# Graph attention on Trainium2: a second of the first projection's seven half-size products also made of seven smaller ones

## The chip, the cores and the metric

The kernel runs on one core of one Trainium2 chip. The metric is the device time of one execution in microseconds (us). Three runs of the kernel before took 2768.26, 2771.11 and 2773.03 us; the median is 2771.11 us.

## What is computed

The reference applies two graph attention layers to 32 graphs of 512 nodes with 512 features, after a layer norm and a relu, and adds the input. The first layer has 4 heads of 256 features that are set side by side (W1 is 512x1024), the second one head of 512 (W2 is 1024x512). All of it is in float32.

```python
def gat_layer(x, mask, W, a_src, a_dst, bias, concat):
    B, N, _ = x.shape
    H, F = a_src.shape
    xl = (x @ W).reshape(B, N, H, F)
    asrc = jnp.einsum('bnhf,hf->bnh', xl, a_src)
    adst = jnp.einsum('bnhf,hf->bnh', xl, a_dst)
    e = jax.nn.leaky_relu(asrc[:, :, None, :] + adst[:, None, :, :], 0.2)
    e = jnp.where(mask[..., None], e, -1e9)
    attn = jax.nn.softmax(e, axis=1)
    out = jnp.einsum('bsdh,bshf->bdhf', attn, xl)
    out = out.reshape(B, N, H * F) if concat else out.mean(axis=2)
    return out + bias

mask = (adj > 0) | eye(512)
h = maximum(layernorm(x), 0)
h = elu(gat_layer(h, mask, W1, att_src1, att_dst1, b1, concat=True))
h = gat_layer(h, mask, W2, att_src2, att_dst2, b2, concat=False)
return x + h
```

## The kernel before

**Sevens.** Each graph has four large products: the first projection (h times W1), the first gather (weights of attention times the projected features, by head), the second projection and the second gather. All but those of the first graph, and the last gather, are done by the scheme of Strassen and Winograd: left and right are cut into 2x2 blocks, sums of blocks are formed, and seven products of blocks take the place of eight. Call the left blocks a11 to a22 and the right ones b11 to b22. The left sums are s1 = a21 + a22, s2 = s1 - a11, s4 = a12 - s2 and a21 = a11 - a21 (in place); the right ones t1 to t4. Product 1 is a11 b11, 2 is a12 b21, 3 is s4 b22, 4 is a22 t4, 5 is s1 t1, 6 is s2 t2, 7 the new a21 times t3. Products that share an output block accumulate in PSUM; a copy by ScalarE or an add by VectorE carries one into another block. The sums of the weights are made once, in `w1_sb` and `w2_sb`; those of the left side for each graph, by VectorE (`sums`, into `hs` and `hs4`).

**The first projection** (`project1`) has four units: two halves of 128 rows in each row block, times two pairs of heads. Per unit and product there are two matmuls, over the two halves of 128 of the block's depth, each with 256 + 2 columns (the two extra ones carry the attention scores). The units are worked on in two groups of two (`ORDER1`), at different places in the program.

**The smaller sevens.** `SMALL = (5,)` names the products of the first projection that are themselves cut into 2x2 and made of seven. Their left blocks are 128x128, their right blocks 128x129, and each small product is one matmul of 129 columns. Product 5 takes 7 matmuls in a group in place of 8 of 258 columns. `small_left` makes the left sums in a buffer `hx` (VectorE, three sums there and one in place), `sums_of_small_weights` the right ones in `wx`, once. `step` in `sevens` emits small product q of one group, in the order 5, 1, 2, 6, 3, 7, 4:

- 5 goes to the upper half of a bank of PSUM that the smalls use by themselves (`tt`), and ScalarE copies it to a buffer `e` (a slot `f`): the shared piece.
- 1 goes to the lower half of that bank, and ScalarE copies it to the first unit's bank; 2 is accumulated there, and 6 on top of 1 in the lower half.
- After 6, VectorE adds the lower half and `e` into the upper half of the first unit's bank, where 3 is accumulated. 7 is accumulated in the lower half, and VectorE adds it and `e` into the second unit's bank. 4 is accumulated in the lower half, and ScalarE copies that to the second unit's bank.

The result of product 5 or 1 is then copied by ScalarE to `xl` or to a second bank, as if it had come from whole matmuls (`done`).

**Order.** `Program` records each operation as a job with its engine, an assumed cost and the keys it reads and writes; from the keys it derives what a job must wait for. The jobs repeat for 30 middle graphs, a "turn" each of 470 jobs: gather 1 and projection 2 of one graph, projection 1 of the next, gather 2 of the one before, and the loads, masks and norm ahead. `PLACES` is a table with a number for each job of the start, of one turn and of the tail. Before, `order` runs a simulation in which each engine takes the ready job with the lowest number, with assumed costs, latencies between engines (`PAIRS`, `CROSS`) and DMA queues that slow each other (`KIND`, `LATE`). The jobs are emitted in the order that comes out, so each engine's sequence is fixed.

**Elsewhere on the way.** `norm` forms the mean and variance of the four tiles of a graph (VectorE), then one POOL power for all four. `norm_turn` applies norm and relu (ScalarE) and turns the tile: for graphs 0 and 1 by TensorE with the identity `identf`, for the others by DMA. The first graph's projection is done plainly (`project1_first`); its weights carry attention scores in two columns, which `scores1` makes with VectorE products from the loads of `att_src1` and `att_dst1` (into `p0`). `xr` is a ring of buffers for the exp of `elu` on ScalarE, which VectorE reads.

Of the kernel before, what the change touches and what calls it, by code (L numbers as in the profile page):

```python
# [10 lines left out]
F32 = mybir.dt.float32  # L11
# [8 lines left out]
P = 128  # L20
EPS = 1e-5
# [23 lines left out]
class Banks(Slots):  # L45
# [171 lines left out]
)  # L217
LATE = {
   
}  # L220


class Program:
# [51 lines left out]
    def kind(self, j):  # L275

        if self.jobs[j][0] == "POOL":
            return self.MASK
# [1431 lines left out]
```

## Time and profile before

| | |
|---|---|
| median of three runs | 2771.11 us (2768.26 to 2773.03) |
| profiled execution, its own time | 2769.33 us |
| its span in the trace | 2767.6 us |
| mean granted clock of TensorE | 0.999 |
| matmuls in the program | 6480, seen as 12924 records |
| operations of VectorE, of ScalarE (records) | 6732, 4907 |
| DMA | 502.14 MB, mean 181 GB/s |

The span runs from the first to the last instruction of the profiled execution. An engine's busy time is the sum over its records, where a float32 matmul shows as two records on TensorE ("PE") with two weight loads ("PEld"). In the groups, a name such as `mm<-wx,hx` reads "to mm, from wx and hx", without the buffers' numbers; L531 is the line of TensorE's helper, L517 that of VectorE's (DVE), L514 that of ScalarE's (ACT). What follows an arrow in a row of idle time is the instruction whose end ended it.

### The profile page before, as it was taken

What the parts mean: (1) busy time and instruction counts of PE and PEld (TensorE: products, weight loads), DVE (VectorE), ACT (ScalarE), POOL (GpSimd) and SP (SyncE); (2) the same over time, 40 slices, a digit from 0 to 9 for tenths busy, and PEclk for the clock granted to TensorE, in tenths of its full rate; (3) what the DMA queues carried; (4) which work ended last, traced back from release to release, by engine and by line L of the source; (5) the groups of instructions that cost most, each with busy time, mean ns of one, the idle gap of its engine ahead of it and who ended that gap; (6) DMA issues with size and microseconds to landing.
All of it is one profiled execution on the core that took longest, in us unless ns stands there. A gap on an engine that the chain in (4) does not pass through costs nothing. (4 is left out here: it accounts for less than half of the span.)

```text
span 2767.6 us, 42320 instructions
## 1 busy us (share of the span) xinstructions
PE 2742.4 (99%) x12924; PEld 2371.8 (86%) x12924; DVE 2558.2 (92%) x6732; ACT 2229.1 (81%) x4907; POOL 313.1 (11%) x356
## 2 busy tenths in 40 slices
PE   7999999999999999999999999999999999999999
PEld 6788888888888888888888888888888888888887
DVE  8999999999999999999999999999999999999996
ACT  5978888778887788877888877888778788788883
POOL 0110111101111111111011111111111111101110
PEclk9999999999999999999999999999999999999999
DMA  8657766667666667667676766766676767767563
GB/s 232 176 157 182 203 167 184 187 176 194 182 183 179 182 176 196 178 175 195 173 201 172 182 187 178 192 186 180 180 188 175 201 167 180 195 165 208 162 171 112
DMA packets 375864, 502.14 MB, mean 181 GB/s; under 512 B 222804, under 2 KB 227668, under 8 KB 375636
## 3 DMA queue, kind: packets, MB, share of 16 engines
q1 hardware_dynamic: 329844, 332.68, 42.4%
q0 software_dynamic: 45792, 166.74, 25.1%
q8 instruction: 103, 1.69, 0.3%
q14 instruction: 125, 1.02, 0.1%
HBM read 316.41 MB, written 51.31 MB: 133 GB/s over the span
## 5 line engine op out<-in xcount | busy, mean ns | idle before, releaser
L531 PE MATMUL mm<-w_sb,hs 128*128 128x257 f32 (+3 forms) x2908 | 667.0, 367 | 5.1 <-ACT mm L514 3.3
L531 PEld LDWEIGHTS mm<-w_sb,hs 128*128 128x128 f32 x2908 | 539.7, 190 | 87.7 <-ACT mm L514 6.7
L525 POOL DMA_DIRECT2D p<-dm x314 | 273.2, 875 | 2295.0 <-DVE p L517 764.3
L531 PE MATMUL mm<-w_sb,ht 128*128 128x258 f32 x2112 | 528.6, 382 | 2.7 <-ACT mm L514 2.5
L531 PE MATMUL mm<-p,xl 128*128 128x258 f32 (+1 forms) x1984 | 495.8, 383 | 0.1
L531 PE MATMUL mm<-w_sb,h 128*128 128x257 f32 x2056 | 477.8, 379 | 0.0
L517 DVE SCALAR_TENSOR_TENSOR p<-rr,z 128x512 f32<-128x512 f32 (+1 forms) x636 | 456.0, 742 | 2.4 <-DMA rr<-drr 2.4
L531 PEld LDWEIGHTS mm<-w_sb,ht 128*128 128x128 f32 x2112 | 393.7, 190 | 63.6 <-ACT mm L514 6.4
L514 ACT ACTIVATE p<-p,z 128x512 f32<-128x512 f32 (+1 forms) x636 | 433.4, 720 | 17.7 <-DVE p L517 12.4
L531 PEld LDWEIGHTS mm<-w_sb,h 128*128 128x128 f32 x2056 | 389.0, 189 | 58.4 <-ACT xl L514 0.5
L531 PEld LDWEIGHTS mm<-p,xl 128*128 128x128 f32 x1984 | 367.2, 190 | 52.7 <-issue 6.0
L514 ACT ACTIVATE mm<-mm 128x257 f32<-128x257 f32 (+2 forms) x498 | 169.8, 347 | 269.2 <-PE mm L531 236.2
L514 ACT ACTIVATE l<-as,z 128x512 f32<-128x512 f32 x516 | 354.4, 716 | 30.8 <-DMA as<-das 30.7
L514 ACT ACTIVATE l<-l,low 128x512 f32<-128x512 f32 x516 | 370.3, 721 | 7.6 <-DVE low L517 6.7
L517 DVE CUSTOM_DVE_ANT_1 l<-l,mt 128x512 f32<-128x512 f32 x516 | 346.2, 681 | 28.4 <-ACT l L514 27.4
L514 ACT ACTIVATE xl<-mm 128x258 f32<-128x258 f32 (+2 forms) x748 | 269.3, 382 | 91.4 <-PE mm L531 89.8
L514 ACT ACTIVATE h<-mm,b_sb 128x256 f32<-128x256 f32 (+1 forms) x504 | 231.0, 480 | 77.3 <-PE mm L531 76.6
L531 PE MATMUL mm<-t,hs 128*128 128x258 f32 (+1 forms) x992 | 246.1, 380 | 0.0
L517 DVE TENSOR_TENSOR xl<-xl,mm 128x258 f32<-128x258 f32 x372 | 155.3, 419 | 57.9 <-PE mm L531 48.3
L531 PEld LDWEIGHTS mm<-t,hs 128*128 128x128 f32 x992 | 185.8, 190 | 25.5 <-DVE t L517 0.2
L531 PE MATMUL mm<-xl,p 128*128 128x258 f32 (+2 forms) x752 | 189.7, 388 | 1.0 <-ACT h L514 0.6
L517 DVE SCALAR_TENSOR_TENSOR h<-xr,h 128x512 f32<-128x512 f32 x256 | 172.2, 683 | 6.1 <-ACT xr L514 6.1
(137 smaller groups left out, 3706.2 us busy)
## 6 DMA issues: line engine op xcount, KB each, us to landing
p<-dm POOLq DMA_DIRECT2D x314, 512.0 KB, 5.0
rr<-drr SPq DMA_DIRECT2D x159, 512.0 KB
x<-in_x_dram SPq DMA_DIRECT2D x129, 256.0 KB
adj<-in_adj_dram SPq DMA_DIRECT2D x128, 256.0 KB
as<-das SPq DMA_DIRECT2D x64, 512.0 KB
t<-in_x_dram SPq DMA_DIRECT2D x124, 256.0 KB
out_dram<-t SPq DMA_DIRECT2D x124, 256.0 KB
dm<-m SPq DMA_DIRECT2D x64, 256.0 KB
```

Source lines behind the costliest of these rows:

```text
L514: prog.add("ACT", cost, reads, writes, lambda: nc.scalar.activation(*a, **k))
L517: prog.add("DVE", cost, reads, writes, lambda: f(*a, **k))
L525: lambda: nc.gpsimd.dma_start(to, at, accum_op=OP.add), size,
L531: f(*a, **k)
```

## The change

Product 1 of the first projection is also made of seven smalls, each of 129 columns (`SMALL = (1, 5)`). Per projection 8 matmuls of 258 columns go and 14 of 129 come. `ORDER1` is unchanged in its text, and gives the smalls of the two products by turns: 5 of product 1, 1 of product 1, 5 of product 5, 1 of product 5, then 2 and 6, 3 and 7, and 4.

Space is found for the second set of buffers in three ways. The shared piece `e` has no slot `f` any more: it is laid in `hx`, where s1 was, once small product 5 has read it. So s1 is formed again (`again`, s2 + a11) between the two groups of a projection. The identity lies in `hx` of product 1 until that product's first sum is made. The ring `xr` has two buffers in place of three. The parts of `hx` have keys of their own.

The norm of the first graph goes tile by tile, with a POOL power for each, where one served all four.

The simulation in `order` is gone: the jobs stand on each engine in the order of their numbers in a new `PLACES`, and a turn has 496 jobs.

```diff
 PLACES = (
-    -21124, -21123, -21187, -21124, -19956, -19941, -19942, -21301, -19903, -19904, -18841, -19897, -6146, 6511,
...
+    -5190682, -5178775, -5187057, -5178772, -5178769, -5191242, -5141726, -5033531, -4987115, -5012829,
...
     def order(self):
-        jobs, rank = self.jobs, self.ranks()
...
+        lines = {e: [] for e in self.ENGINES}
+        for j in sorted(range(len(jobs)), key=lambda j: (rank[j], j)):
+            lines[jobs[j][0]].append(j)
+        lines = [deque(q) for q in lines.values()]
+        while any(lines):
+            q = min((q for q in lines if q and not left[q[0]]), key=lambda q: rank[q[0]])
+            j = q.popleft()
             done.append(j)
...
-    SMALL = (5,)
+    SMALL = (1, 5)
...
-    hx = {n: sbuf.tile([P, 3, P], F32, name=f"hx{n}") for n in SMALL}
+    hx = {n: sbuf.tile([P, 3 * P + 1], F32, name=f"hx{n}") for n in SMALL}
+    identf = hx[SMALL[0]][:, :P]
+    make_identity(nc, identf)
...
-    fs = slots("f", 2, [P, W // 2])
     adjs = slots("adj", 2, [P, N], I32)
-    xrs = slots("xr", 3, [P, N])
+    xrs = slots("xr", 2, [P, N])
...
-        s1, s2, s4 = (hx[n][:, i] for i in range(3))
-        xkeys = [("hx", n)]
-        dve(0.2, keys, xkeys, nc.vector.tensor_add, s1, a21, a22)
-        dve(0.2, keys + xkeys, xkeys, nc.vector.tensor_sub, s2, s1, a11)
+        s2, s4, s1 = (hx[n][:, i * P : (i + 1) * P] for i in range(3))
+        k2, k4, k1 = ([("hx", n, i)] for i in (1, 2, 0))
+        dve(0.2, keys, k1, nc.vector.tensor_add, s1, a21, a22)
+        dve(0.2, keys + k1, k2, nc.vector.tensor_sub, s2, s1, a11)
         dve(0.2, keys, keys, nc.vector.tensor_sub, a21, a11, a21)
-        dve(0.2, keys + xkeys, xkeys, nc.vector.tensor_sub, s4, a12, s2)
+        dve(0.2, keys + k2, k4, nc.vector.tensor_sub, s4, a12, s2)
...
+        def again():
+            dve(0.2, keys + k2, k1, nc.vector.tensor_add, s1, s2, a11)
...
+        for ts in ([t] for t in range(NT)) if b == 0 else [range(NT)]:
+            every = [sk + (t,) for t in ts]
...
-            (tk, tt), (ek, e) = top[n, us], inner[n, us]
+            tk, tt = top[n, us]
+            ek, e = ("hx", n, 0), hx[n][:, 2 * P :]
...
-                fs.give(ek)
+                if us[0] == 0:
+                    small[n].again()
```

**The order on three engines.** In the rows, numbers behind a name are those of one buffer: `mm0` to `mm7` are the eight banks of PSUM, and the rest of the number (`_132`) is not needed. `hx1`, `wx1` belong to product 1, `hx5`, `wx5` to product 5. L531, L517 and L520 of before are L495, L481 and L484 of the change.

TensorE, the first group of smalls of a projection in a middle turn. Before, product 5 alone is of smalls; `w1_sb,ht x2` and `w1_sb,hs x2` are whole products of the projection, `p,xl` belong to the gather:

```order
L531 MATMUL mm0_132<-w1_sb_73,ht_81 128x258 x2
L531 MATMUL mm5_137<-w1_sb_73,hs_83 128x258 x2
L531 MATMUL mm7_139<-wx5_85,hx5_86 128x129
L531 MATMUL mm7_139<-w1_sb_73,hs_83 128x129
L531 MATMUL mm4_136<-p0_102,xl_79 128x256 x2
L531 MATMUL mm2_134<-w1_sb_73,hs_83 128x129
L531 MATMUL mm7_139<-wx5_85,hx5_86 128x129
L531 MATMUL mm5_137<-w1_sb_73,ht_81 128x258 x2
L531 MATMUL mm7_139<-w1_sb_73,hs_83 128x129
L531 MATMUL mm2_134<-w1_sb_73,hx5_86 128x129
```

After the change, from small product 1 of product 1 on (its small product 5 stands before a pair of the gather):

```order
L495 MATMUL mm0_130<-w1_sb_66,ht_74 128x129
L495 MATMUL mm7_137<-wx5_79,hx5_81 128x129
L495 MATMUL mm7_137<-w1_sb_66,hs_76 128x129
L495 MATMUL mm0_130<-wx1_78,hx1_80 128x129
L495 MATMUL mm5_135<-w1_sb_66,ht_74 128x129
L495 MATMUL mm1_131<-w1_sb_66,hs_76 128x129
L495 MATMUL mm7_137<-wx5_79,hx5_81 128x129
L495 MATMUL mm0_130<-w1_sb_66,ht_74 128x129
L495 MATMUL mm5_135<-w1_sb_66,hx1_80 128x129
L495 MATMUL mm1_131<-w1_sb_66,hx5_81 128x129
L495 MATMUL mm7_137<-w1_sb_66,hs_76 128x129
L495 MATMUL mm0_130<-wx1_78,ht_74 128x129
```

Where products of two matmuls stood between the smalls, twelve smalls stand in a row, those in `mm0` and `mm5` of product 1 and those in `mm7` and `mm1` of product 5.

VectorE at the same place; the two adds of product 5 before are `mm<-mm,f0`:

```order
L517 TENSOR_TENSOR ht_81<-ht_81 128x2x256
L517 TENSOR_SCALAR m_105<-adj0_94 128x512
L517 TENSOR_TENSOR p2_104<-p2_104 128x2x256
L517 TENSOR_TENSOR mm2_134<-mm7_139,f0_92 128x129
L517 TENSOR_TENSOR x0_88<-xl2_80,x1_89 128x2x256
L517 TENSOR_SCALAR m_105<-adj1_95 128x512
L517 TENSOR_TENSOR mm1_133<-mm7_139,f0_92 128x129
```

After, with the sums s4 (`hx<-ht,hx`, `hx<-hs,hx`) and four adds `mm<-mm,hx`:

```order
L481 SCALAR_TENSOR_TENSOR h1_75<-xr0_95,h1_75 128x512
L481 TENSOR_TENSOR t3_107<-p2_102 128x512
L481 TENSOR_TENSOR hx1_80<-ht_74,hx1_80 128x128
L481 TENSOR_TENSOR mm5_135<-mm0_130,hx1_80 128x129
L481 TENSOR_TENSOR hx5_81<-hs_76,hx5_81 128x128
L481 TENSOR_TENSOR mm1_131<-mm7_137,hx5_81 128x129
L481 TENSOR_TENSOR mm2_132<-mm0_130,hx1_80 128x129
L481 SCALAR_TENSOR_TENSOR p0_100<-rr1_113,z1_124 128x512
L481 TENSOR_SCALAR m_103<-adj0_93 128x512
L481 TENSOR_TENSOR mm3_133<-mm7_137,hx5_81 128x129
```

The sums s4 now stand between and just ahead of the adds after small product 6, and the first three adds are close to each other.

SP's queue at the start: the weights, the four tiles of graph 0 and the two vectors of scores. Before:

```order
L520 DMA w1_sb_73<-in_L0_gnn_W1_dram 128x2x256
L520 DMA x2_90<-in_x_dram 128x512
L520 DMA x0_88<-in_x_dram 128x512
L520 DMA x3_91<-in_x_dram 128x512
L520 DMA x1_89<-in_x_dram 128x512
L520 DMA p0_102<-in_L0_gnn_att_src1_dram 128x512
L520 DMA w1_sb_73<-in_L0_gnn_W1_dram 128x2x256 x3
L520 DMA p0_102<-in_L0_gnn_att_dst1_dram 128x512
L520 DMA w1_sb_73<-in_L0_gnn_W1_dram 128x2x256 x3
```

After:

```order
L484 DMA w1_sb_66<-in_L0_gnn_W1_dram 128x2x256
L484 DMA x0_89<-in_x_dram 128x512
L484 DMA x2_91<-in_x_dram 128x512
L484 DMA x1_90<-in_x_dram 128x512
L484 DMA x3_92<-in_x_dram 128x512
L484 DMA w1_sb_66<-in_L0_gnn_W1_dram 128x2x256
L484 DMA p0_100<-in_L0_gnn_att_src1_dram 128x512
L484 DMA w1_sb_66<-in_L0_gnn_W1_dram 128x2x256
L484 DMA p0_100<-in_L0_gnn_att_dst1_dram 128x512
L484 DMA w1_sb_66<-in_L0_gnn_W1_dram 128x2x256 x5
```

The second vector (`att_dst1`) is the ninth load and was the tenth, and the weights stand partly ahead of the first vector and mostly behind the second.

More of the change, by code (lines that the diff above doesn't have):

```diff
@@ L305, in order @@
                 after[d].append(j)
-        left = [len(job[2]) for job in jobs]
-        ready_at, self.start, done = [0.0] * n, [0.0] * n, []
-        free, soon, ready = dict.fromkeys(self.ENGINES, 0.0), defaultdict(list), defaultdict(list)
-        wires, now, behind = {"SP": deque(), "POOL": deque()}, 0.0, {"SP": 0.0, "POOL": 0.0}
-        for j in range(n):
-            if not left[j]:
-                heappush(soon[jobs[j][0]], (0.0, j))
-        def release(j, at):
-            for s in after[j]:
-                ready_at[s] = max(ready_at[s], at(s))
-                left[s] -= 1
-                if not left[s]:
-                    heappush(soon[jobs[s][0]], (ready_at[s], s))
@@ L321, in step @@
-        def step(until):
-            nonlocal now
-            busy = [q for q in wires if wires[q] and wires[q][0][1] <= now]
-            speed = dict.fromkeys(wires, 1.0)
-            if len(busy) == 2:
-                speed["SP"], speed["POOL"] = self.kind(wires["SP"][0][0])[2:]
-            event, which = until, None
-            for q in wires:
-                if wires[q]:
-                    j, since, todo = wires[q][0]
-                    t = now + todo / speed[q] if q in busy else since
-                    if t < event:
-                        event, which = t, q
-            for q in busy:
-                wires[q][0][2] -= (event - now) * speed[q]
-                behind[q] -= (event - now) * speed[q]
-            now = event
-            if which in busy:
-                j = wires[which].popleft()[0]
-                release(j, lambda s: event + self.kind(j)[1] + LATE.get(self.place[j], 0) / 100)
-            return which is not None
@@ L371, in order @@
+        for j in sorted(range(len(jobs)), key=lambda j: (rank[j], j)):
[4 more added lines that the diff above has]
+            j = q.popleft()
+            done.append(j)
+            for k in after[j]:
+                left[k] -= 1
         return done
@@ L603, in operands @@
             return lefts[q], (right, w1_keys(n - 1) + [("wx", n)])
+        operands.again = again
         return operands
```

104 lines of the change are left out of this document (23 added, 81 removed), and 357 rows, old and new, of the table PLACES.

## The prediction

> **What bounds the kernel now.** I read the page's first part, then busy time by stage, the waits of TensorE, and its timeline. From the page:
>
> ```profile
> span 2767.6 us, 42320 instructions
> PE 2742.4 (99%) x12924; PEld 2371.8 (86%) x12924; DVE 2558.2 (92%) x6732; ACT 2229.1 (81%) x4907; POOL 313.1 (11%) x356
> ```
>
> Three stages (columns: the stretch, its length, busy us and instructions of PE, PEld, DVE, ACT, POOL, the granted clock, the DMA share, GB/s):
>
> ```profile
> 0.00:70.00 70.00, 55.45 (x262) 47.77 (x263) 58.09 (x239) 39.83 (x92) 4.79 (x10) 0.98 0.81 231
> 1400.00:1800.00 400.00, 400.00 (x1913) 349.77 (x1912) 374.26 (x974) 331.74 (x726) 45.13 (x51) 1.00 0.69 183
> 2700.00:2768.00 68.00, 63.88 (x264) 49.26 (x262) 43.40 (x110) 21.38 (x49) 1.75 (x2) 0.99 0.33 106
> ```
>
> TensorE is busy for the whole of the middle stage, at full granted clock. Of the 25.2 us that it lacks to the span, 14.55 lie in the first 70 us and 4.1 in the last 68. Its longest waits over the whole span (total, times, longest):
>
> ```profile
> PE mm L531 <- ACT x L514: 12.1, 1, 12.1
> PE mm L531 <- ACT mm L514: 5.8, 10, 1.2
> PE mm L531 <- DVE hs L517: 1.3, 1, 1.3
> ```
>
> and its only wait between 600 and 2100 us:
>
> ```profile
> PE mm L531 <- ACT mm L514: 3.2, 5, 1.2
> ```
>
> So the kernel is as long as TensorE's matmuls plus one start and one tail. Every matmul taken out counts, and so does every new wait. VectorE stands next: 374.26 of 400 us.
>
> **What is removed and added on TensorE.** A trace record is half a matmul here (12924 records, 6480 matmuls in the program). In TensorE's timeline (start, length):
>
> ```profile
> 1011.07 2.77 PE L531 MATMUL mm<-w_sb,ht 128*128 128x258 f32 x12
> 1013.68 1.03 PE L531 MATMUL mm<-t,hs 128*128 128x256 f32 x4
> 1014.54 0.39 PE L531 MATMUL mm<-wx,hx 128*128 128x129 f32 x2
> 1014.76 0.39 PE L531 MATMUL mm<-w_sb,hs 128*128 128x129 f32 x2
> 1014.99 1.03 PE L531 MATMUL mm<-t,hs 128*128 128x258 f32 x4
> ```
>
> Twelve records of 258 columns take 1013.68 - 1011.07 = 2.61 us from start to start, 0.2175 each, so 0.435 for a matmul. A small one of 129 columns takes 0.22 or 0.23 to the next start, 0.225 over the two. Each of the 31 projections drops 8 matmuls of 258 columns and gains 14 of 129: 8 x 0.435 - 14 x 0.225 = 0.33 us, or 0.40 with 0.22. I take the middle, 0.365: 31 x 0.365 = 11.3 us less (bounds 10.2 and 12.4).
>
> **What the smalls wait for.** Seven smalls are a chain: the result of 1 is copied by ScalarE before 2 and 6 may write, that of 6 is added by VectorE before 3 and 7 run, that of 7 before 4. Before, products of 0.87 us stood between most of these steps. Now, in the first of a turn's two groups, twelve smalls of products 1 and 5 stand directly behind each other (the order rows in the section on the change), so that two or three others, 0.45 or 0.67 us, stand between a step and what it needs. How long such a copy and such an add are (mean ns after the busy us):
>
> ```profile
> L514 ACT ACTIVATE mm<-mm 128x129 f32<-128x129 f32 x124 | 32.6, 263 | 8.1 <-PE mm L531 8.1
> ```
>
> ```profile
> L517 DVE TENSOR_TENSOR mm<-mm,f 128x129 f32<-128x129 f32 x124 | 36.6, 295 | 2.5 <-PE mm L531 2.5
> ```
>
> And a handover in each direction, from the timeline:
>
> ```profile
> 1014.75 0.47 ACT L514 ACTIVATE h<-mm,b_sb 128x256 f32<-128x256 f32 x1 [0.45 <-PE mm L531]
> ```
>
> ```profile
> 1025.43 0.52 ACT L514 ACTIVATE mm<-mm 128x129 f32<-128x129 f32 x2
> 1025.73 0.19 PEld L531 LDWEIGHTS mm<-w_sb,ht 128*128 128x128 f32 x1 [0.35 <-ACT mm L514]
> ```
>
> The matmuls at 1013.68 end at 1014.71, and ScalarE starts 0.04 later; the first of the two copies from 1025.43 ends near 1025.69, and TensorE goes on 0.04 later. A small is 0.39 long, so from its start to that of its dependant go 0.39 + 0.04 + 0.26 + 0.04 = 0.73 us by ScalarE, and 0.39 + 0.04 + 0.295 + 0.04 = 0.765 by VectorE. In the order rows small 1 of product 1 (first row) is three starts ahead of its 6 (fourth), as is 1 of product 5 (third) of its 2 (sixth), and 6 of product 5 (seventh) of its 3 (tenth): 3 x 0.222 = 0.67 us. These copies lack 0.06 each and the add 0.10. The add of product 1 has four starts (fourth to eighth row), 0.89, and lacks nothing. Low bound: one wait, 0.06 us per turn, since TensorE's wait for one product is room for the other. High bound: all three, 0.22. I take 0.15, the middle: 31 x 0.15 = 4.7 us (bounds 2 and 7). The second group keeps products of 0.86 us between its steps and is costed at nothing; without that cover it would cost as much as the first.
>
> **What is added on the other engines.** Per projection four VectorE sums for the left side, two repeated sums (the shared piece is laid where that sum was) and four adds from PSUM, and six ScalarE copies. One of the existing left sums, and two VectorE operations in a row:
>
> ```profile
> L517 DVE TENSOR_TENSOR hx<-hs 128x128 f32<-128x128 f32 x31 | 8.8, 285 | 0.0
> ```
>
> ```profile
> 1020.83 0.69 DVE L517 TENSOR_TENSOR p<-p,t 128x512 f32<-128x512 f32 x1
> 1021.43 0.75 DVE L517 SCALAR_TENSOR_TENSOR p<-rr,z 128x512 f32<-128x512 f32 x1
> ```
>
> At most 6 x 0.285 + 4 x 0.295 = 2.9 us of VectorE per turn. Where the next operation starts 0.09 before the end of the one ahead, as at 1021.43, it is 10 x 0.09 less, 2.0. A turn is about 85 us (2600 us for thirty turns and a half), in which VectorE has 85 x 25.7 / 400 = 5.5 us free; it keeps 2.6 to 3.5. ScalarE gains 6 x 0.263 = 1.6 us and has 85 x 68.3 / 400 = 14.5 free. Both stay hidden behind TensorE as long as their order meets TensorE's, and cost nothing; uncovered, VectorE's part would cost 31 x 2.9 = 90 us. The buffers for ScalarE's exp go from three to two. An exp that waits for VectorE holds up what stands behind it on ScalarE, the copies from PSUM among them; before, such waits were:
>
> ```profile
> ACT xr L514 <- DVE h L517: 5.1, 5, 1.3
> ```
>
> I put this at nothing out of the 14.5 us, bounds 0 and 5 (as much again, all of it passed on).
>
> TensorEngine Tiling (Array Packing) in the Trainium skill, section PSUM Bottleneck, warns that TensorE can be sped up without PSUM being emptied any faster, so that the copies become the bottleneck. The trace agrees that VectorE is near it (374.26 of 400).
>
> **Start and tail.** The start:
>
> ```profile
> 12.06 2.82 PE L531 MATMUL mm<-identf,x 128*128 128x128 f32 x12 [12.06 <-ACT x L514]
> ...
> 13.21 0.43 DVE L517 SCALAR_TENSOR_TENSOR xr<-w_sb,p 128x256 f32<-128x256 f32 x1 [1.30 <-DMA p<-in_L_gnn_att_dst_dram]
> ...
> 14.67 5.92 PE L531 MATMUL mm<-w_sb,ht 128*128 128x258 f32 x24
> ```
>
> The norm of the first graph now goes tile by tile, so the first transpose need not wait for the fourth load. But the first projection, at 14.67, waits for the scores in the weights, whose last four VectorE products begin at 13.21 with the tenth load of SP's queue (0.365 us each up to 14.67). In the new queue the tenth load is a piece of the weights, and two products are left behind it: 0.7 us earlier. Bounds: 0, if the loads come later, and 2.6 us (14.67 - 12.06), if they no longer bind. I take 0.7. The first smalls of graph 1 come where VectorE is still at the sums:
>
> ```profile
> 46.94 1.14 PE L531 MATMUL mm<-w_sb,ht 128*128 128x258 f32 x4 [0.53 <-ACT mm L514]
> 49.40 1.65 PE L531 MATMUL mm<-w_sb,hs 128*128 128x258 f32 x4 [1.32 <-DVE hs L517]
> ...
> 54.44 0.49 PE L531 MATMUL mm<-w_sb,hs 128*128 128x129 f32 x2 [0.46 <-DVE mm L517]
> ```
>
> Product 1 in whole was the cover there; without it these 2.3 us may come once more. I put nothing, bounds -1 and +3. The tail keeps its matmuls and adds and is put at nothing.
>
> **Sum.** The profiled execution took 2769.3 us for its span of 2767.6. 2769.3 - 11.3 + 4.7 - 0.7 = 2762.0. The median of the runs, 2771.1, lies 1.8 above that execution, so 2763.8, say 2764.
>
> **Rivals.** *VectorE late in the group* (the other side). With half its idle time gone, VectorE enters the group of twelve behind by one operation of 128x512 in each turn; at its first add the next small and all of TensorE behind it wait. Price, the 0.69 of the row at 1020.83: 31 x 0.69 = 21.4, so 2785. It takes the gain away from 0.365 us of waits per turn on, and shows as slower from 0.365 + 5.5 / 31 = 0.54. For it: 5.5 us free fall to about 3, and in VectorE's new order the adds follow straight on sums and on each other. Against it, VectorE's waits from 1400 to 1800 us:
>
> ```profile
> DVE xl L517 <- PE mm L531: 7.6, 15, 0.9
> ```
>
> It is ahead of TensorE three times per turn, and the new order has no long operation between the group's first three adds.
>
> *Only handed back*: the group's waits at their high end, 0.22 us per turn, and the exp buffers at theirs, 5 us: 2763.8 + 31 x 0.07 + 5 = 2771, no change. For it: the three places are there in the order, and the ring is shorter. Against it: two products that never overlap, and every wait of an exp passed on.
>
> *Weight loads bind*: each small loads its own 128x128 weights, for half the columns (min/median/max of one load in ns):
>
> ```profile
> L531 PEld LDWEIGHTS mm<-wx,hx x4: 190/190/190, 1014.3 to 1016.9; 128*128 128x128 f32 x4
> ```
>
> If a run of twelve went at 0.190 per record, not at 0.111, it would cost 12 x 2 x 0.079 x 31 = 59 us: 2823. Against it: the two smalls at 1014.54 stand in a row, and start 0.22 apart. Perfetto Trace Analysis in the Trainium skill, section Matmuls, holds larger matmuls to be more efficient than smaller ones where there is a choice. The trace does not bear it out at this size: 0.2225 against 0.435 is 51% of the time for half the columns.
>
> **How the numbers follow.** Forecast, 2764: chance 0.46. Its own range is 2757 to 2766; the lower end is 2769.3 - 12.4 + 2 - 2.6 + 1.8 = 2758 less a run's spread. Handed back: 0.25. VectorE late: 0.25. Weight loads: 0.04. A measurement of this kernel tells about 0.2%, 5.5 us, from no change; so faster is under 2765.6, slower over 2776.6, with 0.46, 0.25 and 0.29. The range goes from 2757 to 2786, the price of late VectorE; worse lateness and the weight loads are left out.
>
> **What would show it.** TensorE's busy time falls from 2742 to about 2735, with 372 records more; starts of the twelve smalls lie 0.22 apart but for two or three gaps of 0.05 to 0.1 in each turn. VectorE's share from 1400 to 1800 us rises from 94% to 96 or 97%. TensorE's waits for "mm" by ScalarE or VectorE rise from 6 us to some 11. The first projection starts near 14.0. I am wrong if these waits grow beyond 17 us (VectorE late), if smalls start 0.3 apart with both engines long done (weight loads), or if the gaps lie elsewhere in the turn, which would be the new order and not the smalls.

## The result and the profile after

The change takes 2807.09 us (median of 4 runs, 2803.35 to 2809.28), the kernel before 2769.69 beside it: 1.0136 times as long, interval 1.0114 to 1.0157. So it is slower, by 37 us, and above the predicted range. Single executions that took far longer than the others of their kernel (one of e1 with 5888.85 us, one of e12 with 4187.2, two of the kernel before with 2864.19 and 2866.26) do not enter the ratios, and as e1's was its profiled one, e1 has no trace to read. The profiled execution of the change took 2808.66 us. Its page begins:

```profile
span 2806.9 us, 43903 instructions
PE 2762.8 (98%) x13296; PEld 2382.8 (85%) x13296; DVE 2630.4 (94%) x7052; ACT 2270.2 (81%) x5093; POOL 318.2 (11%) x359
```

TensorE has the 372 records more that the change adds, and 11 us less of matmul to do, yet is busy for 20 us longer. The first and the middle stage (columns as before):

```profile
0.00:70.00 70.00, 52.66 (x248) 45.31 (x249) 53.53 (x213) 32.46 (x74) 5.30 (x12) 0.95 0.66 200
1400.00:1800.00 400.00, 397.20 (x1931) 345.78 (x1930) 380.70 (x1011) 332.48 (x741) 47.78 (x53) 1.00 0.69 183
```

In the middle stage TensorE lacks only 2.8 of 400 us. The busy column hides the loss; the distance between equal rows does not. One small product of the first group, in an early and a late turn of TensorE's timeline, before:

```profile
164.40 0.39 PE L531 MATMUL mm<-wx,hx 128*128 128x129 f32 x2
...
2631.54 0.39 PE L531 MATMUL mm<-wx,hx 128*128 128x129 f32 x2
```

and after the change:

```profile
325.78 0.39 PE L495 MATMUL mm<-wx,hx 128*128 128x129 f32 x2
...
2563.55 0.39 PE L495 MATMUL mm<-wx,hx 128*128 128x129 f32 x2
```

Before, these are 29 turns, 85.07 us each; the shortest, which come again and again, are 84.68, and the rest, 0.39 a turn, is losses scattered over some turns. After, they are 26 turns of 86.07, nearly all of 86.04. The mean turn is longer by 1.00, or 29 us in 29 turns; the other 10 of the span's 39.3 lie at the start and the tail. Against the shortest turn before, the change is 1.36 longer, though its matmuls are 0.365 shorter: about 1.7 us are lost in each turn. Most of them are found in the first group, TensorE's timeline:

```profile
1445.07 0.39 PE L495 MATMUL mm<-wx,hx 128*128 128x129 f32 x2
1445.30 1.03 PE L495 MATMUL mm<-p,xl 128*128 128x256 f32 x4
1446.76 0.49 PE L495 MATMUL mm<-w_sb,ht 128*128 128x129 f32 x2 [0.43 <-ACT hx L478]
1447.08 0.39 PE L495 MATMUL mm<-wx,hx 128*128 128x129 f32 x2
1447.31 0.39 PE L495 MATMUL mm<-w_sb,hs 128*128 128x129 f32 x2
1447.60 0.49 PE L495 MATMUL mm<-wx,hx 128*128 128x129 f32 x2
1447.92 0.39 PE L495 MATMUL mm<-w_sb,ht 128*128 128x129 f32 x2
1448.15 0.39 PE L495 MATMUL mm<-w_sb,hs 128*128 128x129 f32 x2
1448.37 0.39 PE L495 MATMUL mm<-wx,hx 128*128 128x129 f32 x2
1448.77 0.49 PE L495 MATMUL mm<-w_sb,ht 128*128 128x129 f32 x2
1449.10 0.61 PE L495 MATMUL mm<-w_sb,hx 128*128 128x129 f32 x4
1449.55 0.39 PE L495 MATMUL mm<-w_sb,hs 128*128 128x129 f32 x2
1449.77 0.39 PE L495 MATMUL mm<-wx,ht 128*128 128x129 f32 x2
1450.01 1.14 PE L495 MATMUL mm<-w_sb,ht 128*128 128x258 f32 x4
```

Read the starts, not the idle times. Without a wait the next start comes 0.87 us after a pair of whole matmuls and 0.22 after a small:

- **W1.** 1446.76 should be 1446.17: 0.59 late. The view calls only 0.43 idle, since successive matmuls overlap by 0.17. This is small 1 of product 1.
- **W2.** 1447.60 (its small 6) should be 1447.53: 0.07 late, and no idle time at all.
- **W3.** 1448.77 (its small 7) should be 1448.59: 0.18.
- **W4.** The whole pair at 1450.01 is 0.02 late at most, but it is recorded with 1.14 like the products that waited.
- **Restarts.** A product that had to wait is recorded longer (0.49 for 0.39, 1.14 for 1.03), and the next starts 0.32 behind a small, not 0.22, and 0.97 behind the pair, not 0.87. So each wait costs 0.10 more, and it counts as busy.

This makes 0.59 + 0.07 + 0.18 + 4 x 0.10 = 1.24 in the first group. In the second:

```profile
1474.05 1.03 PE L495 MATMUL mm<-w_sb,ht 128*128 128x258 f32 x4
1475.22 0.49 PE L495 MATMUL mm<-wx,hx 128*128 128x129 f32 x2
1475.55 0.39 PE L495 MATMUL mm<-w_sb,hs 128*128 128x129 f32 x2
```

**W5.** 1475.22 (small 6 of product 5) should be 1474.92: 0.30, and 0.10 for the restart. Together 1.64, against the 1.7 of the turns.

What was late? ScalarE at W1, in its timeline:

```profile
1444.70 1.32 ACT L478 ACTIVATE p<-p,z 128x512 f32<-128x512 f32 x2
1445.93 0.61 ACT L478 ACTIVATE xr<-h 128x512 f32<-128x512 f32 x1
1446.45 0.26 ACT L478 ACTIVATE hx<-mm 128x129 f32<-128x129 f32 x1
```

Small 5 of product 1 (the row at 1445.07) was done at 1445.46, but its copy `hx<-mm`, the shared piece, stands on ScalarE behind an operation of the softmax and an exp of `elu`, and ends at 1446.71; small 1 starts 0.05 later. It does not read that piece. It writes the other half of the same bank of PSUM. VectorE before W3:

```profile
1448.42 0.30 DVE L481 TENSOR_TENSOR mm<-mm,hx 128x129 f32<-128x129 f32 x1 [0.78 <-PE mm L495]
```

VectorE had been idle for 0.78 us: it was not late. The add needs small 6, which ended at 1448.09 (1447.60 + 0.49), yet it starts 0.11 behind the end of the next product of TensorE, small 2 (1447.92 + 0.39 = 1448.31). Small 2 writes one half of the bank whose other half the add writes (`mm5` in the order rows of the section on the change), and the wait listed for the add is the one for small 2. Before, such an add started 0.04 behind its small 6 (at 1427.66, behind 1427.62). So W3, like W1, is not a wait for the data; no run tests it alone. W2 is one (small 6 goes 0.06 behind the end of the copy of 1), and W4 (0.06 behind the copy that its product is added to).

And ScalarE at W5:

```profile
1474.41 0.56 ACT L478 ACTIVATE mm<-mm 128x129 f32<-128x129 f32 x2
1474.87 0.30 ACT L478 ACTIVATE hx<-mm 128x129 f32<-128x129 f32 x1
```

Small 6 needs the first of these three copies, which ends about 1474.67, and goes on after the last, at 1475.17.

The waits of TensorE's two rows over the span, and ScalarE's wait for the exp ring:

```profile
PE mm L495 <- ACT hx L478: 16.7, 31, 2.7
```

```profile
PEld mm L495 <- ACT hx L478: 44.8, 61, 2.9
```

```profile
ACT xr L478 <- DVE h L481: 83.4, 33, 3.1
```

The matmuls' row shows one wait per turn and the loads' row two: the idle time ahead of a load is longer (0.83 at W1 where the matmul's is 0.43), so that W5 shows there too. The exp waits rose from 5.1 to 83.4 us.

### The profile page after: what moved, and what is told of

Read it like the earlier page. It is cut to its first block, busy times and chain, and to the rows that moved or that the text cites. A ratio compares the mean times of both kernels' runs of the same rounds, so it can differ in the third digit from the quotient of the medians.

```text
span 2806.9 us, 43903 instructions
## 1 busy us (share of the span) xinstructions
PE 2762.8 (98%) x13296; PEld 2382.8 (85%) x13296; DVE 2630.4 (94%) x7052; ACT 2270.2 (81%) x5093; POOL 318.2 (11%) x359
## 4 chain that ended last, share of the span: by engine, by line
PE 80%; ACT 12%; DVE 5%; issue 2%; DMA 1%; SPq 0%; ACTq 0%; DVEq 0%
PE mm L495 80%; ACT p L478 3%; ACT l L478 2%; ACT xr L478 2%; ACT h L478 2%; ACT mm L478 1%; DVE l L481 1%; DVE hs L481 1%; DVE p L481 1%; DVE t L481 1%; ACT xl L478 1%; DMA p<-dm 1%; ACT hx L478 0%; ACT x L478 0%; DVE stats L481 0%
## 5 line engine op out<-in xcount | busy, mean ns | idle before, releaser
L495 PE MATMUL mm<-w_sb,hs 128*128 128x257 f32 (+2 forms) x2908 | 672.1, 367 | 0.8 <-ACT mm L478 0.4
L495 PEld LDWEIGHTS mm<-w_sb,hs 128*128 128x128 f32 x2908 | 534.1, 190 | 75.7 <-ACT h L478 4.6
L495 PE MATMUL mm<-p,xl 128*128 128x258 f32 (+1 forms) x1984 | 505.8, 383 | 1.3 <-ACT p L478 0.9
L495 PE MATMUL mm<-w_sb,ht 128*128 128x258 f32 (+1 forms) x1988 | 485.6, 367 | 16.6 <-ACT hx L478 16.0
L495 PE MATMUL mm<-w_sb,h 128*128 128x257 f32 x2056 | 468.9, 379 | 0.0
L481 DVE SCALAR_TENSOR_TENSOR p<-rr,z 128x512 f32<-128x512 f32 (+1 forms) x636 | 448.8, 741 | 2.1 <-DMA rr<-drr 2.1
L495 PEld LDWEIGHTS mm<-w_sb,h 128*128 128x128 f32 x2056 | 388.9, 189 | 58.6 <-ACT mm L478 0.7
L478 ACT ACTIVATE p<-p,z 128x512 f32<-128x512 f32 (+1 forms) x636 | 424.8, 713 | 11.8 <-DVE p L481 9.1
L495 PEld LDWEIGHTS mm<-w_sb,ht 128*128 128x128 f32 x1988 | 353.1, 191 | 73.5 <-ACT hx L478 27.7
L495 PEld LDWEIGHTS mm<-p,xl 128*128 128x128 f32 x1984 | 364.6, 190 | 53.0 <-issue 6.0
L481 DVE CUSTOM_DVE_ANT_1 l<-l,mt 128x512 f32<-128x512 f32 x516 | 342.3, 683 | 1.0 <-ACT l L478 0.7
L478 ACT ACTIVATE mm<-mm 128x257 f32<-128x257 f32 (+2 forms) x622 | 202.5, 334 | 164.2 <-PE mm L495 155.9
L478 ACT ACTIVATE xl<-mm 128x258 f32<-128x258 f32 (+2 forms) x748 | 262.9, 378 | 68.9 <-PE mm L495 58.7
L495 PE MATMUL mm<-t,hs 128*128 128x258 f32 (+1 forms) x992 | 246.2, 380 | 2.5 <-DVE xl L481 1.5
L478 ACT ACTIVATE xr<-h 128x512 f32<-128x512 f32 x256 | 161.0, 630 | 84.3 <-DVE h L481 83.4
L495 PEld LDWEIGHTS mm<-t,hs 128*128 128x128 f32 x992 | 185.7, 190 | 28.8 <-DVE t L481 2.1
L495 PE MATMUL mm<-xl,p 128*128 128x258 f32 (+2 forms) x752 | 194.5, 388 | 1.5 <-ACT p L478 1.5
L481 DVE SCALAR_TENSOR_TENSOR h<-xr,h 128x512 f32<-128x512 f32 x256 | 174.1, 682 | 1.2 <-ACT xr L478 1.2
```

The costliest lines, as they stand in the source:

```text
L478: prog.add("ACT", cost, reads, writes, lambda: nc.scalar.activation(*a, **k))
L481: prog.add("DVE", cost, reads, writes, lambda: f(*a, **k))
L495: f(*a, **k)
```

## The experiments

**Theory A** came from the instructions' listed waits. The jobs of all engines are recorded one after another into one program (`emit`), and that order is more than the sequences of the single engines: an instruction can only be made to wait for what is recorded ahead of it. Two operations of different engines on one bank are kept in the order in which they are recorded, also where they use different halves; operations of one engine that are recorded in a row give one signal, after the last (the listings show this, not the trace). Before, the jobs were recorded in the order of simulated time. The change takes any job that is ready, lowest number first, and so records ScalarE's and VectorE's far ahead of TensorE's: the copy of small 5 ahead of small 1 (W1), three copies in a row ahead of small 6 (W5), the third of which reads the other half of small 6's bank. TensorE's listing of the change, from the pair of the gather at 1445.30 to small 6 (`Activation` is ScalarE):

```
692 L495 MATMUL mm_137<-p_100,xl 128x256 [waits DVE_49]
693 L495 MATMUL mm_137<-p_100,xl 128x256
694 L495 MATMUL mm_133<-w_sb,ht 128x129 [waits Activation_49]
695 L495 MATMUL mm_131<-wx_79,hx_81 128x129
696 L495 MATMUL mm_131<-w_sb,hs 128x129
697 L495 MATMUL mm_133<-wx_78,hx_80 128x129 [waits Activation_49]
```

Small 1 (694) has a wait on ScalarE that the data does not ask for.

The Trainium skill, PSUM — Partial Sum Buffer, section "PSUM bank collisions raise a hardware error", asks for two engines to be kept apart by bank, whatever the addresses. The listed wait of small 1 on a copy of the bank's other half agrees; no run here shows a collision.

**Theory B**: the chain of the smalls itself is too dense, or an engine is late in itself: ScalarE behind its exps, or VectorE (the prediction's rival). **Theory C**: the weight loads of the smalls bind. **Theory D**: the new order is slower, whatever the smalls.

All results, with the ratio to the before beside it and the median distance of one small product from turn to turn in the profiled execution:

| kernel | us | ratio (interval) | turn, us |
|---|---|---|---|
| before | 2765.2 to 2769.7 | 1 | 84.98, shortest 84.68 |
| the change | 2807.09 | 1.0136 (1.0114 to 1.0157) | 86.04 |
| e5 the change again | 2806.03 | 1.0147 (1.0132 to 1.0162) | 86.03 |
| e1 | 2791.47 | 1.0096 (1.0078 to 1.0114) | |
| e2 | 2804.36 | 1.0142 (1.0126 to 1.0158) | 86.00 |
| e7 | 2798.61 | 1.012 (1.0103 to 1.0137) | 85.74 |
| e3 | 2788.07 | 1.0085 (1.0069 to 1.0101) | 85.52 |
| e4 | 2788.44 | 1.0084 (1.0068 to 1.01) | 85.42 |
| e6 | 2786.11 | 1.0074 (1.0059 to 1.0089) | 85.46 |
| e8 | 2793.39 | 1.01 (1.0085 to 1.0115) | 85.70 |
| e9 | 2770.90 | 1.0017 (1.0009 to 1.0026) | 84.89 |
| e10 | 2774.39 | 1.0036 (1.0023 to 1.0049) | 85.10 |
| e11 | 2778.54 | 1.0048 (1.0034 to 1.0061) | 85.12 |
| e12 | 2763.81 | 0.9989 (0.998 to 0.9998) | 84.62 |
| e13 | 2769.09 | 1.0012 (1.0003 to 1.0021) | 84.85 |

**e1: four copies recorded behind small 1.** Every engine's own sequence is unchanged.

```diff
+PLACES = list(PLACES)
+for _v, _p in (
+    (127, 1413266), (129, 1413267), (131, 1413269), (133, 1413268),
+):
+    PLACES[1209 + _v] = _p
```

> Every engine keeps its sequence of instructions; only the order in which the jobs are recorded across engines changes: in each of the 28 middle turns small 1 of product 1 is recorded ahead of ScalarE's copy of small 5 (both use one bank of PSUM), so that it has no wait for that copy. Theory A (the wait is made by the recorded order and by nothing the computation needs): the 0.60 us of waiting and the 0.10 us of slower restart go, and small 6 waits about 0.07 us more for its own copy: 28 x 0.63 = 17.6 us less, about 2789 us (2786 to 2793). Theory B (ScalarE is late, behind the exps of a shorter ring, and TensorE is held at the next small in any case): the wait moves to small 6 whole, 2803 to 2807 us. Theory C (weight loads of the smalls bind): no change, 2807 us.

In the listing the wait of small 1 is gone:

```
694 L500 MATMUL mm_133<-w_sb,ht 128x129
695 L500 MATMUL mm_131<-wx_79,hx_81 128x129
696 L500 MATMUL mm_131<-w_sb,hs 128x129
697 L500 MATMUL mm_133<-wx_78,hx_80 128x129 [waits Activation_49]
```

And 2806 (e5) becomes 2791.5, inside the range: 15 us, of the 28 x 0.69 = 19 that W1 is worth. Only the recording changed, so this much of the loss is neither the smalls' density nor a late ScalarE. The rest is probably a longer W2, as e3 shows it below; e1 has no trace that could tell.

**e2: small 6 of the second group recorded ahead of the two copies that follow; e7: also the copy of small 5 ahead of the copy of 1.** The lines that differ, of e2 and then of e7:

```diff
+    (274, 1685761), (276, 1685762), (282, 1685764), (298, 1685763),
...
+    (274, 1685761), (275, 1687026), (276, 1685762), (277, 1687028), (282, 1685764), (298, 1685763),
```

> Every engine keeps its sequence. In the second group of smalls of a middle turn, small 6 of product 5 is recorded right behind ScalarE's copy of small 1, ahead of the two copies that follow on ScalarE and which were recorded together with it. Theory A (copies recorded in a row give one signal, at the last of them): small 6 no longer waits until the third copy ends; 0.30 us of waiting and 0.10 of restart per turn go, 28 x 0.4 = 11 us less, 2796 us (2793 to 2800). Theory B (ScalarE is late in itself): the copy of small 1 ends no earlier and TensorE starts no earlier, 2805 to 2808 us.

> The changed kernel; in the second group, ScalarE makes the copy of small 5 of product 5 ahead of that of its small 1 (the two change places), and small 6 is recorded right behind both and ahead of the next copy. In the run before with small 6 recorded ahead, the copy of small 5 was recorded behind small 6 and had to wait for it, as they share a bank; here neither waits for the other. Theory A: 0.30 us of waiting and most of the 0.10 of restart go in each of 28 turns: 10 us less than the change, 2796 us (2792 to 2799). Theory B (ScalarE is late in itself and the wait goes elsewhere): 2802 to 2808 us.

e2 missed: the turn fell by 0.04, not by 0.4. ScalarE's timeline in e2:

```profile
1472.84 0.28 ACT L483 ACTIVATE hx<-mm 128x129 f32<-128x129 f32 x1 [0.37 <-PE mm L500]
```

Now the copy of small 5 is recorded behind small 6, which uses its bank, and has to wait for it: the bank's order was turned round, and the wait moved to ScalarE and on to what stands behind. Small 6 itself starts on time, but at four places behind it TensorE's starts lose 0.36 in each turn. In e7 that copy goes first, and the turn falls to 85.74: W5's 0.30 is gone, and the time is inside the range. Its restart stays, since small 6 still waits for a copy that has just ended. Whether W5 came from the common signal or from the third copy's use of small 6's bank, e2 and e7 do not tell; both lie in the recorded order.

**e3: everything recorded by time.** The engines' sequences as in the change, the recording by a plain simulation:

```diff
     def order(self):
...
-        return done
+        at, end, free = {}, {}, dict.fromkeys(self.ENGINES, 0.0)
+        for j in done:
+            e, cost, deps = jobs[j][:3]
+            at[j] = max([free[e], *(end[d] for d in deps)])
+            free[e] = at[j] + cost
+            end[j] = free[e] + (2.0 if e in ("SP", "POOL") else 0.15)
+        return sorted(done, key=at.get)
```

> Every engine keeps its sequence; all jobs are recorded in the order of their starts in a simple sum of costs along each engine and each dependency. Theory A: both waits above go at once, also those of graph 1 at the start (some 3 us): 17.6 + 11 + 3 = 32 us less, 2775 us (2770 to 2783). What is left over the kernel before is the chain of smalls in the first group (0.45 us per turn). Theory B or C: 2800 to 2808 us.

It missed its range (2770 to 2783): of the 31 us from 2806 to 2775, 18 came. The same place on TensorE:

```profile
1433.92 0.39 PE L501 MATMUL mm<-w_sb,ht 128*128 128x129 f32 x2
1434.15 0.39 PE L501 MATMUL mm<-wx,hx 128*128 128x129 f32 x2
1434.37 0.39 PE L501 MATMUL mm<-w_sb,hs 128*128 128x129 f32 x2
1434.85 0.49 PE L501 MATMUL mm<-wx,hx 128*128 128x129 f32 x2
```

W1 is gone (0.22 behind small 1), but W2 grew from 0.07 to 0.26: the copy of 1 now queues behind the same exp, so W2 takes over a part of what W1 had waited out. W3 and W5 stay as they were. The recording explains W1; the plain simulation did not mend W5.

**e6: the kernel before, recorded early.** The cross-check: all of before's own sequences, but the jobs of every engine other than TensorE recorded up to 30 places ahead.

```diff
+        key = {j: i + (0 if jobs[j][0] == "PE" else -30) for i, j in enumerate(done)}
+        q = min((q for q in lines if q and not left[q[0]]), key=lambda q: key[q[0]])
...
-        for j in self.order():
+        for j in self.early():
```

> The kernel before, every engine with its own sequence as it was; only the jobs of ScalarE, VectorE and the queues are recorded up to 30 jobs earlier against TensorE's. In one group of smalls per projection ScalarE's copy of small 5 then stands recorded ahead of small 1, which stands directly behind small 5 on TensorE, and small 1 gets a wait for it that it did not have. Theory A (recorded order makes the waits): small 5 to its copy's end is 0.39 + 0.04 + 0.26 + 0.04 = 0.73 us where 0.22 was, and 0.10 of restart: 0.6 us per projection, 31 x 0.6 = 19 us more, and up to twice that where the copy stands behind an exp: 2785 us (2778 to 2805). Theories B, C and D (lateness of an engine, weight loads, the sequence): nothing changes, 2765 to 2771 us.

As forecast: 2786.11, 21 us above before, from nothing but the recording. TensorE's timeline shows the wait that it made:

```profile
1446.64 0.39 PE L548 MATMUL mm<-wx,hx 128*128 128x129 f32 x2
1447.54 0.49 PE L548 MATMUL mm<-w_sb,hs 128*128 128x129 f32 x2 [0.51 <-ACT f L531]
1447.86 1.03 PE L548 MATMUL mm<-t,hs 128*128 128x258 f32 x4
```

Small 1 of product 5 starts 0.90 behind small 5 in place of 0.22, and a restart of 0.10 follows: 0.78, the very difference of the turns (85.46 less 84.68).

**e4: product 1 whole, in the change's order and recording.** The whole products of product 1 stand at the places of its smalls 2 and 3.

```diff
-    SMALL = (1, 5)
+    SMALL = (5,)
```

> Product 1 is whole again (8 matmuls of 258 columns in place of 14 of 129, without its sums, copies and adds); the order of all that is left, the buffers and the norm stay as in the change, and its two whole products per group stand where smalls 2 and 3 of product 1 stood. Theory A (the time was lost at the smalls of product 1 and what waits for them): nearly all waits of the middle turns go, 46 us, and 11 us of matmuls come back: 2772 us (2767 to 2779). Theory D (the new order as such, with the shorter ring for exp, is slower): 2785 to 2810 us.

**e5: the change once more**, for the spread from chip to chip.

> The changed kernel itself, beside the runs that follow: 2800 to 2810 us.

e5 agrees with the change. e4 missed by 16 us: 0.46 stood at W5's small in each turn (0.35 and a restart), and 0.27 at the gather (0.17 and a restart) was new. That looked like theory D, and e8, e9 and e11 followed.

**e8: recorded by time, and eight jobs of the group moved** to give the first group's copies and adds room (four copies of ScalarE, two sums and one 128x512 operation of VectorE, one small of TensorE).

> The jobs recorded by time as before, the two copies of the second group changed as in the run ahead, and three moves in the first group of a middle turn: small 1 of product 1 directly behind its small 5 on TensorE, its copy ahead of that of small 5 on ScalarE, and on VectorE the sums s4 ahead of, and the long difference t1 behind, the adds of the smalls. Theory A: of the 1.18 us of waits per turn left in the run recorded by time, the 0.36 at small 6 of the first group and the 0.40 in the second go, and about 0.1 of the 0.28 at small 7: 28 x 0.86 = 24 us less than that run's 2788, 2764 us (2759 to 2772). Theory B (VectorE cannot take the difference later): waits for t or h take their place, 2780 us or more.

It missed by 29 us. VectorE in e8, and TensorE at that place:

```profile
1447.00 0.68 DVE L493 TENSOR_TENSOR t<-p,t 128x512 f32<-128x512 f32 x1
```

```profile
1446.48 1.03 PE L507 MATMUL mm<-p,xl 128*128 128x256 f32 x4
1447.73 1.13 PE L507 MATMUL mm<-t,hs 128*128 128x256 f32 x4 [0.23 <-DVE t L493]
```

The pair at 1447.73 should start at 1447.35; it waits for an operation that VectorE ends at 1447.68. Here VectorE is late, which it was not in the change: with 19 us of 400 left it has little room. Which of the eight moves made it late was not separated.

**e9: product 1 whole in the first group, of smalls in the second; e11: product 1 whole in both.** Both are recorded by time, with e7's swap of the two copies and one 128x512 operation of VectorE earlier.

```diff
-            (n, v, q) for qs in ((5, 1), (2, 6), (3, 7), (4,)) for n in SMALL for q in qs
+            (n, v, q) for qs in ((5, 1), (2, 6), (3, 7), (4,)) for n in SMALL[u == 0 :] for q in qs
```

> Product 1 is of smalls only in the second group of a projection, where gather products stand between the smalls; in the first group it is whole, and its left sums are made after that group. Recorded by time, with the copies of the second group as in the run with the copy of small 5 ahead, and with one difference t on VectorE ahead of three masked scores. Theory A: the run with product 1 whole took 2788 us, with 0.74 us of waits per turn; about 0.13 stay, 28 x 0.61 = 17 us less; some 3 us less at the start; 4 matmuls of 258 fewer and 7 of 129 more per projection, 31 x 0.18 = 5.7 us less: 2763 us (2758 to 2770), no slower than the kernel before. Theory D (the new sequence as such is slower): 2775 us or more.

> Product 1 whole in both groups, recorded by time, with the same two changes to the second group's copies and to t. Theory A: the waits of the run with product 1 whole (0.46 at a small of product 5, 0.28 at t, per turn) came from the recorded order and from the place of t: 2788 - 17 - 3 = 2768 us (2763 to 2774). Theory D (the new sequence as such is slower): 2780 us or more.

Both came out slower than expected, e9 by 8 us and e11 by 10.5. Of the wait at W5's small little more than the restart was left, and the one at the gather was still there. ScalarE in e9:

```profile
1409.13 1.35 ACT L477 ACTIVATE ht<-x 128x1024 uint16<-128x1024 uint16 x1
...
1410.61 0.38 ACT L477 ACTIVATE mm<-mm 128x256 f32<-128x256 f32 x1
```

The last copy, for which the gather waits, stood behind `ht<-x` of 1.35 us. The cause was the edit: `ranks` adds the sum of TensorE's assumed costs in a turn to the numbers of the next one, and whole products have another sum (84.4 to 84.6 in place of 84.23), so that jobs of neighbouring turns changed places. e4's sum is 84.57 as well.

**e12 and e13: e9 and e11 with that sum held.**

```diff
-        turn = sum(job[1] for job in self.jobs[first : first + each] if job[0] == "PE")
+        turn = 84.22698847667229
```

> The run with product 1 whole in the first group, with the length of a turn, by which the places of the next turn are shifted, kept at the change's 84.23 (it is a sum of TensorE's costs and had risen with the whole products). That puts a copy of ScalarE for the gather ahead of a copy of ht and one of xl again, as in the change. Theory A: the wait of 0.18 + 0.10 us per turn at the gather goes, 28 x 0.28 = 8 us less than 2771: 2763 us (2759 to 2768). Theory D (the new sequence as such is slower): 2769 us or more.

> Product 1 whole in both groups, recorded by time, with the length of a turn kept in the same way. Theory A: the wait at the gather (0.45 and 0.26 us in two turns looked at) goes, some 9 us less than 2778.5: 2769 us (2765 to 2774); what is left over the kernel before lies at the start and the end. Theory D: 2775 us or more.

Both hit. e12's middle stage:

```profile
1400.00:1800.00 400.00, 399.95 (x1943) 350.70 (x1942) 382.70 (x1010) 332.80 (x741) 44.81 (x50) 1.00 0.68 182
```

TensorE is full again, with the change's new order, its tile-by-tile norm, its ring of two (84.6 us of exp waits) and VectorE busier than in the change (382.70). So theory D falls: with product 1 whole (e13) all that is new costs 3.5 us in this form. And smalls pay where they have cover: from e13 to e12 half of the change's smalls come in, and the time falls by 5.3 us, 0.23 per turn. e12 is the only version below before, by 0.1%, too little to call it faster.

**e10: smalls of product 1 in both groups, with the best of the rest.** Recorded by time, smalls 5 and 1 of product 1 side by side ahead of the gather's pair, and e9's other moves.

```diff
+    (127, 1360695), (128, 1403132), (129, 1357851), (221, 1452873), (275, 1687026), (277, 1687028),
```

> The run recorded by time and moved, without its two moves on VectorE in the first group, and with one difference t ahead of three masked scores. Theory A: the 0.39 + 0.10 us of waiting for t in that run came from the moves and goes; left per turn are 0.22 at small 6, 0.28 at small 7, 0.1 and 0.1: 0.7 us against 1.18 in the run recorded by time, 28 x 0.45 = 12.6 us less than 2788: 2775 us (2770 to 2781). Theory B (VectorE is the bound between the first group and the differences): 2785 us or more.

As forecast: 33 us of the loss are recovered. What is left against e12, 10.6 us and 0.48 in a turn, lies in the first group:

```profile
1426.06 0.39 PE L506 MATMUL mm<-w_sb,hs 128*128 128x129 f32 x2
1426.41 0.49 PE L506 MATMUL mm<-wx,hx 128*128 128x129 f32 x2
...
1427.18 0.39 PE L506 MATMUL mm<-wx,hx 128*128 128x129 f32 x2
1427.59 0.49 PE L506 MATMUL mm<-w_sb,ht 128*128 128x129 f32 x2
```

W2 (0.35 for 0.22) and W3 (0.41 for 0.22) with two restarts: 0.13 + 0.19 + 0.20 = 0.52. W4's restart adds 0.10, and e10's other half of the smalls takes 0.18 away. This is not plain density. The copy of 1 ends at 1426.16, and small 6 (1426.41) could go at 1426.28; it goes 0.05 behind the end of the copy of small 5 (1426.10 + 0.26), which uses its bank and is recorded ahead of it, as in W1. And W3's add starts at 1427.23, again 0.10 behind the end of small 2 (1426.74 + 0.39). No run took these two away.

## Why the prediction was wrong

**What bounds the kernel** was right: TensorE stayed the bound, and every wait it was given was paid in full.

**Matmuls taken out, 11.3 us.** Right. (In each group 7 smalls take the place of 4 matmuls of 258 columns, not of 8 as the section on the kernel before says; the prediction counts rightly.) The smalls start 0.22 apart wherever nothing is waited for, and half of them brought 5.3 us (e12 against e13) where half of 11.3 is 5.65. The rival "weight loads bind" falls with this.

**The step that failed is "What the smalls wait for", 4.7 us with bounds 2 and 7.** It measured about 1.65 us per turn, 46 us in 28 turns, for three reasons:

- It listed only the waits that the data asks for. Of its three places one waited, small 6 of product 1 (W2, priced at 0.06, measured 0.07); the other two waited for nothing. W1 (0.59) is none of them: small 1 needs nothing from the copy of small 5; it waits since both use a bank and the copy is recorded first. The diff showed the simulation that set this order being taken out, and the prediction priced only the engines' sequences. e1 and e6 show this cause alone, in both directions.
- The add of product 1 "has four starts" and "lacks nothing", but W3 (0.18) is there: the add followed small 2, one start later than small 6. And the second group, "costed at nothing" under its products of 0.86 us, lost 0.40: not the copy that was needed but the last of three was waited for (e7).
- Each wait costs a restart of 0.10, five in a turn, and no term has it. The rows that show a restart stand in the prediction itself: 0.49 for a small at 54.44 behind a wait, 0.39 elsewhere. TensorE's busy time, in which restarts count, rose to 2762.8, where a fall to about 2735 was the sign of the forecast.

The sum with what was measured: 46 us of waits, less 11 of matmuls, less 10 of scattered losses that the kernel before had and the change has not (0.36 in a turn), and 10 at the start and the tail make 35, of the 37 measured. W1's cause is shown by experiment, and that of W5 but for the choice above; W3's is read from the trace and the listing only.

**VectorE and ScalarE hidden, ring of two at nothing.** Right. VectorE's share from 1400 to 1800 us is 95.2% (96 or 97 forecast). ScalarE waits 78 us more for the exp ring, but TensorE is full in e12 with the same ring and the same waits.

**Start and tail.** The first projection starts later, not earlier, and the first smalls cost more. TensorE's timeline of the change:

```profile
14.50 1.11 PE L495 MATMUL mm<-hx,x 128*128 128x128 f32 x4 [0.83 <-ACT x L478]
15.40 22.97 PE L495 MATMUL mm<-w_sb,ht 128*128 128x258 f32 x96
...
48.44 0.49 PE L495 MATMUL mm<-wx,hx 128*128 128x129 f32 x2 [1.14 <-ACT ht L478]
51.65 0.80 PE L495 MATMUL mm<-w_sb,ht 128*128 128x129 f32 x2 [2.72 <-ACT hx L478]
...
62.10 1.36 PE L495 MATMUL mm<-w_sb,ht 128*128 128x129 f32 x6 [1.58 <-ACT hx L478]
```

15.40 is 0.7 later than before, where 0.7 earlier was forecast: the fourth transpose stands directly ahead and waits for ScalarE's part of the norm, so the load of the scores no longer binds. The projection is slower at first, too: from 16 to 18 us TensorE makes 7 records, before 11, and its 96 records take 22.96 us to the next start, 2.1 more than at 0.2175 each, where the 24 of before lost 0.5. The granted clock reads 1.00 there in both, so why stays open. The waits shown at 48 to 62 us add up to 5.4, where the prediction's three rows add up to 2.3; the bound was +3. And at the tail, put at nothing, TensorE's last 32 records wait 1.47 us for ScalarE, before for nothing.

**Rivals.** "VectorE late" gave 2785 and the right sign, but not the mechanism: VectorE was idle before the add. "Only handed back" took the same three places at their high end, and two of them did not wait.

**What stays open.** Of the 10 us outside the 29 turns some 7 are named (0.7, 1.5, 3.1 and 1.5 in the order above); norm and ring were not tried alone, nor W3.

## What to carry to other kernels

Where jobs are recorded into one program, the recording order across engines is part of the schedule: compare the listed waits of each instruction before and after, not only each engine's sequence, and look first at operations that share a bank without sharing data. Measure a periodic kernel by the distance of one instruction from turn to turn; it showed 1.36 us where the busy shares showed 99% and 100%. When an edit changes an assumed cost, hold everything that is derived from it, or the experiment tests two things.

## What the runs showed of the hardware

A wait of TensorE costs 0.10 us beyond its length: the product behind it is recorded at 0.49 us in place of 0.39 and the next one starts 0.32 later rather than 0.22 (the rows of the change, e3, e6 and e10). The loads show what differs: the load of a small stands 0.11 ahead of its product elsewhere (1447.81 for the small at 1447.92), and with a product that waited it starts at the same time (1448.77). And in the 2.72 us wait at the start the granted clock fell, from 1.00 between 49 and 50 us to 0.51 between 50 and 51; the windows of the change and the timeline:

```profile
52.00:57.00 5.00, 4.63 (x22) 4.34 (x22) 2.35 (x7) 1.15 (x4) 0.00 (x0) 0.52 0.96 331
```

```profile
55.12 0.64 PE L495 MATMUL mm<-wx,hx 128*128 128x129 f32 x2
55.55 0.64 PE L495 MATMUL mm<-w_sb,ht 128*128 128x129 f32 x2
```

At a granted clock of 0.52 smalls start 0.43 apart, twice the usual 0.22, and all of it counts as busy. The Trainium skill, TensorE: Matmul & The Clock Gate, Part 1, has TensorE at half clock after an idle window of about 3.4 us, until it has been busy for about as long. The trace agrees in the clock, not in the idle time: the fall came within a wait of 2.72, and in the kernel before behind waits of only 0.53 and 1.32 (0.50 from 50 to 53 us). The smalls ran slowly from 51.65 to 56.84, 5.2 us with a second wait of 0.37 among them.
